# Two-layer graph kernel: the end of the last graph, with its roots regrouped and the work of the graph before moved forward

## The chip, the core and the metric

The kernel runs on one core of a Trainium2 chip. The metric is the device time of one execution in microseconds (us); lower is better. The core has five engines with queues of their own, each working through its queue in order: TensorE (PE, matrix products; PEld is its loading of weights), VectorE (DVE), ScalarE (ACT), GpSimd (POOL) and SyncE (SP, which here issues DMAs). They wait for each other by semaphores.

## The reference, cut to what matters

There are 16 graphs of 1024 nodes with 256 features. Two layers follow each other, and both end in a residual addition and a layer norm over the 256 features of a node. What matters for the change is the second layer's end and the layer norm:

```python
def _layernorm(x, axis=-1, eps=1e-5):
    m = jnp.mean(x, axis=axis, keepdims=True)
    v = jnp.var(x, axis=axis, keepdims=True)
    return (x - m) / jnp.sqrt(v + eps)
...
    Hh = jnp.einsum('bni,io->bno', h, W)
    logits = s[:, :, None] + d[:, None, :]
    e = jnp.where(adj != 0, jnp.exp(-leaky_relu(logits)), 0)
    rowsum = jnp.sum(e, axis=-1, keepdims=True)
    h_prime = jnp.einsum('bnm,bmo->bno', e, Hh) / rowsum
    return jax.nn.elu(h_prime)
...
x = _layernorm(x + _L0_gnn_ref(...))
x = _layernorm(x + _L1_gnn_ref(...))
```

So each output row is the norm of `x1 + elu(sum / rowsum)`, where `x1` is the row after the first layer.

## The kernel before, in words

The rows of a graph are eight tiles of 128. The kernel works through the graphs in a pipeline: while graph `b` runs through its first layer, the second layer of graph `b - 1` (`prev`) is finished, and the normed rows of graph `b - 2` (`done`) are scaled and stored. The schedule is written by hand (`tc.manual_schedule()`): each engine gets its instructions in the order in which the Python code emits them. This holds for the DMA queues too, since a DMA is issued in its place in an engine's queue.

A tile of the second layer passes through these steps. `sum1` (L654) accumulates the product of the weights `e` with `H` on TensorE, with the sum of a row's weights as a last column. `elu` takes its reciprocal on VectorE (L690, L691), and ScalarE makes the positive part (L699) and the exponential (L700). `add` joins both (L705) and adds `x1` (L707 for most graphs, L712 for graph 15), both on VectorE. Then the mean and the variance are needed. For most graphs the mean comes out of the addition, and `deviation1` has ScalarE sum the squares (L364). For graph 15, the last one, VectorE takes statistics of the row (`stats`: L346 and L348).

`center` makes the factor `r = 1/sqrt(v + eps)` and the offset `mr = -mean * r` for several tiles at once on GpSimd, in one batch of eight instructions: the sum with eps (L356 or L358), a power of -0.5 (L377), a Newton step of four instructions (L380 to L383), and the offset in two (L393, L394). `scale1` then has ScalarE scale a tile (L399), and `store` writes tiles out (L727) from SyncE's queue, or ScalarE's where it says so.

The end of the program begins in the last round of the loop (`last`, with `b` = 15 and `prev` = 14). There the eight tiles of graph 14 are summed; after tile 7's sums the weights of graph 15 for its first four tiles of rows are made on VectorE (`weights`, L649), eight of 128x512 followed by eight more for the second half. Then follow graph 15's own sums: the first four tiles together, over `m` from 0 to 7 (`acc_15_0` to `acc_15_3`), then tiles 4, 5 and 6, and last tile 7 in two halves of columns (L1046). Within this stretch VectorE adds tile 7 of graph 14, ScalarE takes the last two deviations, and GpSimd makes all eight roots of graph 14 (`center(mv1s[done])`). The eight scalings of graph 14 are spread, two after each of graph 15's tiles 2 to 5.

The tiles of graph 15 are rooted in this way: tiles 0 to 2 in one batch on GpSimd after tile 3's sums (code of `t == 4`), tiles 3 to 5 in a second batch (`t == 5`), and tiles 6 and 7 at the very end by a square root on ScalarE (L992) and a reciprocal with a Newton step on VectorE (L997 to L1002), which then also scales both tiles (L1119). The square root belongs to another set of activation tables than the exponentials, so ScalarE loads one ahead of it.

The kernel counts on all values of `adj` being 0 or 1 and on sums within limits. A flag is computed on the way (L1087), each engine loads it into a register (L1094), and a branch on it (L1463) decides between a general path, which does not run with these inputs, and the last store: tiles 6 and 7 of graph 15 from `y_last` (L1467, SyncE). After it all engines meet to close the program (L1501).

Of the kernel before, what the change touches and what calls it, by code (L numbers as in the profile page):

```python
# [18 lines left out]
P = 128  # L19
# [11 lines left out]
def one_kind_pass(  # L31
# [312 lines left out]
    def stats(y, mv, what):  # L344
        st = small.tile([P, nc.vector.BN_STATS_DIM], F32, tag="st", name=f"st_{what}")
        nc.vector.bn_stats(st, y)  # L346
        if mv is not None:
            nc.vector.bn_aggr(mv, st)  # L348
        return st
# [38 lines left out]
    def center(mv, what, add_eps=EPS, unit=1.0):  # L388

        r = rstd(mv, what, add_eps, unit)  # L390
        n = mv.shape[1]
        mr = small.tile([P, NT], F32, tag="mr", name=f"mr_{what}")[:, 0:n]
        nc.gpsimd.tensor_tensor(mr, mv[:, :, 0], r, ALU.mult)  # L393
        nc.gpsimd.tensor_scalar(mr, mr, -unit, None, ALU.mult)  # L394
        r_all[what] = r
        return [(r[:, t : t + 1], mr[:, t : t + 1]) for t in range(n)]
# [240 lines left out]
    def check_pq(b):  # L637
        near = small.tile([P, 2, NT], F32, tag="near", name=f"near_{b}")
        nc.vector.tensor_scalar(near, pqs[b], LOW, 1.0 / LOW, ALU.max, ALU.min)
        nc.vector.tensor_tensor(near, near, pqs[b], ALU.is_equal)  # L640
        nc.vector.tensor_reduce(fit[:, b : b + 1], near, AX.XY, ALU.min)

    def weights(b, m, t0=0, n=NT):

        if m == 0 and t0 == 0:
            es[b] = one.tile([P, NT, N], F32, tag="ew" if b < B - 1 else "al", name=f"e_{b}")
        cols = ds(t0 * P, n * P)
        q, e, rows = pqs[b][:, 1, m : m + 1], es[b][:, m, cols], adjs[b, m // HT][:, m % HT, cols]
        nc.vector.scalar_tensor_tensor(e, p_bcs[b][:, cols], q, rows, ALU.mult, ALU.min)  # L649
# [3 lines left out]
    def sum1(b, t, acc, m):  # L653
        nc.tensor.matmul(  # L654
            acc,
            lhsT=es[b][:, m, ts(t, P)],
            rhs=Hs[b][m],
            start=(m == 0),
            stop=(m == NT - 1),
        )  # L660
# [41 lines left out]
    def add(b, t, between=None):  # L702

        y = ys[b][t]
        nc.vector.scalar_tensor_tensor(y, y, 1.0, hs[b, t], ALU.min, ALU.add)  # L705
        if b < B - 1:
            nc.vector.scalar_tensor_tensor(  # L707
                y, y, -1.0, x1s[b][:, t, :], ALU.add, ALU.add, accum_out=mv1s[b][:, t, 0:1]
            )
            return None  # L710
        if (b, t) != (B - 1, NT - 2):
            nc.vector.scalar_tensor_tensor(y, y, -1.0, x1s[b][:, t, :], ALU.add, ALU.add)  # L712
        if between:
            between()

        full = (b, t) == (B - 1, NT - 2)
        return stats(y, None if full else mv1s[b][:, t, :], f"1_{b}_{t}")

    def deviation1(b, t):
        deviation(ys[b][t], mv1s[b][:, t, :])  # L720
# [82 lines left out]
    for b in range(1, B):  # L803
# [127 lines left out]
        for t in range(NT):  # L931
            if t == 6 and not last:
                add(prev, t - 1)
                deviation1(prev, t - 2)
                strip(b + 1, 0)
                finish(b + 1, 0, ends=False)
                dump(b + 1, 0)
            if t >= n_first:
                acc = sum_of(t)
                for m in range(NT):  # L940
                    sum1(prev, t, acc, m)
            if last and t == 7:
                for m in range(4):
                    weights(b, m, 0, HT)
            elu(prev, t, *((first[t], rinvs[t]) if t < n_first else (acc,)))
            if last and t in (2, 3):
                for q in range(HT):
                    stats0(b, (t - 2) * HT + q)
                roots0(b, t - 2)
            if t >= 1 and (last or t != 6):  # L950
                add(prev, t - 1)
            if t >= 2 and (last or t != 6):
                deviation1(prev, t - 2)
            if not last and t in (3, 5):
                sums0(b, (t - 3) // 2)
                if t == 5:
                    load_adj(b + 1, 1, behind=mv0s[b][:, HT, 0:1])
            if not last and t >= 4:
                for q in range(2 * t - 8, 2 * t - 6):
                    deviation0(b, q)  # L960
                if t % 2 == 1:
                    roots0(b, (t - 5) // 2)
            for n in ([0], [1], [2, 3])[t - 5] if not last and t >= 5 else []:
                combine_x(b + 1, n)
            if t == 3 and not last:
                scale_x(b + 1, 0)
                scale_x(b + 1, 1)
            if last and t in (4, 6):
                t0 = (t - 4) // 2 * HT
                for n in range(HT):  # L970
                    project(b, t0 + n)
                evict_H()
                save_p(b, t0, HT, nc.gpsimd)
                share_p(b, t0, HT)
            if last and t in (5, 7):
                for q in range(HT):
                    scale0(b, (t - 5) // 2 * HT + q)
            if last and t == 7:
                for m in range(4, 6):
                    weights(b, m, 0, HT)  # L980
# [4 lines left out]
    last, done = B - 1, B - 2  # L985
    r1s[last] = []

    def root(t, st):

        nc.vector.bn_aggr(mv1s[last][:, t, :], st)  # L990
        r = roots_sb[:, t - (NT - 2) : t - (NT - 2) + 1]
        nc.scalar.activation(r, mv1s[last][:, t, 1:2], AF.Sqrt, bias=eps)  # L992

    def invert_roots():

        v, r = mv1s[last][:, NT - 2 :, 1], roots_sb
        nc.vector.reciprocal(r, r)  # L997

        n = const.tile([P, 2], F32, tag="newton", name="newton")
        nc.vector.scalar_tensor_tensor(n, v, EPS, r, ALU.add, ALU.mult)  # L1000
        nc.vector.scalar_tensor_tensor(n, n, -0.5, r, ALU.mult, ALU.mult)
        nc.vector.scalar_tensor_tensor(r, n, 1.5, r, ALU.add, ALU.mult)  # L1002
        return r

    roots_sb = const.tile([P, 2], F32, tag="root", name="root")
    n_first = 4
    first = [acc1(last, t, *((ps_e, "e") if t < 3 else (ps_t, "t"))) for t in range(n_first)]
    for m in range(NT):
        if m in (3, 4):
            weights(last, m + 3, 0, HT)  # L1010
        if m == 4:
            add(done, NT - 1)
            for q in (NT - 2, NT - 1):
                deviation1(done, q)
            r1s[done] = center(mv1s[done], f"1_{done}", unit=1.0 / D)

        for k in range(3 * m - 15, min(3 * m - 12, NT)) if m >= 5 else []:
            weights(last, k, HT, HT)
        for t in range(n_first):
            sum1(last, t, first[t], m)  # L1020
    check_pq(last)

    n_chk, n_fit = chk.shape[1], fit.shape[1]
# [51 lines left out]
    for t in range(end):  # L1075
        if n_first - 1 <= t < end - 1:
            multiply1(t + 1)
        if t == 5:
            multiply_halves()
        if t == 4:  # L1080
            total = ps_t.tile([P, HT, P], F32, tag="t", name="total")[0:1, 0, 0:1]
            nc.tensor.matmul(total, lhsT=any_bad, rhs=ones, start=True, stop=True)
        elu(last, t, accs[t])
        if 1 <= t < 6:
            add(last, t - 1)
        if t == 5:
            nc.vector.tensor_copy(flag, total)  # L1087
            add(last, t)
        if t == 6:
            st_full = add(last, t, invert)  # L1090
        if t in (4, 5):
            r1s[last] += center(mv1s[last][:, ds(3 * t - 12, 3), :], f"1_{last}_{t}")
        if t == 5:
            n_bad = nc.values_load(  # L1094
                flag, min_val=0, max_val=P, skip_runtime_bounds_check_because="a number of partitions"
            )
        for q in range(2 * t - 4, 2 * t - 2) if 2 <= t < 6 else []:
            scale1(done, q)
            if q in (3, 7):
                store(done, q - 3, HT)  # L1100
        if t == 5:
            for q in range(3):
                scale1(last, q)
            store(last, 0, 3)
    h_end = two.tile([P, D], F32, tag="h", name="h_end")
    st_end = two.tile([P, 2, nc.vector.BN_STATS_DIM], F32, tag="low", name="st_end")
    end_half(0)
    scale1(last, 3)
    scale1(last, 4)
    store(last, 3, 2)  # L1110
    end_half(1)
    root(end, st_end)
    root(end - 1, st_full)
    r = invert_roots()
    scale1(last, 5)
    store(last, 5, 1, nc.scalar)
    for q in (6, 7):
        y = ys[last][q]
        nc.vector.tensor_scalar(  # L1119
            y, y, mv1s[last][:, q, 0:1], r[:, q - 6 : q - 5], ALU.subtract, ALU.mult  # L1120
        )
    return n_bad


# [380 lines left out]
```

## Time and profile before

| | |
|---|---|
| time, median of 3 runs | 1214.67 us (1214.66 to 1217.69) |
| the profiled execution's own time | 1215.24 us |
| its span, from first to last instruction | 1213.4 us |
| TensorE busy | 1202.4 us, 99% of the span |
| VectorE, ScalarE, GpSimd busy | 83%, 69%, 32% |
| TensorE's last product ends | 1205.1 us |
| the last store is issued (L1467) | 1209.42 us |
| mean granted TensorE clock | 0.998 |

The page gives the busy time of each engine, the span in 40 slices, and the chain of work that ended last. The timeline of one engine lists its instructions in order of time: start, duration, engine, line, operation, what it writes and reads, how often (xN), and in brackets the idle time before it with what ended it. The answer for one source line lists its instructions by queue (POOLq is GpSimd's instruction queue, which also takes the waits and branches), with the shortest, median and longest duration in ns, and when the first and the last of them start.

### The profile page before, as it was taken

To read this page: it belongs to the slowest core of one execution; us is meant where nothing else is said; L and a number is where in the kernel's file an instruction comes from. 1 tells how busy PE (TensorE), PEld (TensorE's weight loads), DVE (VectorE), ACT (ScalarE), POOL (GpSimd) and SP (SyncE) were. 2 spreads that over 40 slices of the span, in tenths; PEclk is the share of its full clock that TensorE was granted. 3 is DMA by queue.
4 is the path that set the end of the run, shared out by engine and by line. 5 is a ranking of instruction groups with operands and counts; after the bars stand their busy time and mean duration, and the time that the engine had idled before them with its cause. 6 is when DMAs were issued, how large, how long until landed. Compare 5 with 4: busy or idle time off the path is not lost.

```text
span 1213.4 us, 16001 instructions
## 1 busy us (share of the span) xinstructions
PE 1202.4 (99%) x4369; PEld 817.5 (67%) x4369; DVE 1005.8 (83%) x1778; ACT 833.2 (69%) x2133; POOL 391.2 (32%) x716
## 2 busy tenths in 40 slices
PE   9999999999999999999999999999999999999997
PEld 6757657576575766758667586775757657576686
DVE  5798896987979789797897978979798896988956
ACT  4574767767677666875768757786676767767674
POOL 3310433504334142431414324143250433404343
PEclk9999999999999999999999999999999999999999
DMA  9778788696887878788687886978869788687412
GB/s 201 150 147 156 131 157 171 132 190 127 149 176 135 184 146 154 157 144 182 139 176 134 153 183 129 182 138 155 174 131 190 129 154 172 133 188 135 112 49 73
DMA packets 613913, 182.51 MB, mean 150 GB/s; under 512 B 490164, under 2 KB 596280, under 8 KB 613816
## 3 DMA queue, kind: packets, MB, share of 16 engines
q1 hardware_dynamic: 591632, 138.74, 57.4%
q0 software_dynamic: 20528, 41.95, 18.6%
q8 instruction: 37, 0.61, 0.2%
q10 hardware_dynamic: 1656, 0.72, 0.2%
q14 instruction: 60, 0.49, 0.2%
HBM read 153.36 MB, written 61.54 MB: 177 GB/s over the span
## 4 chain that ended last, share of the span: by engine, by line
PE 93%; DVE 2%; DMA 2%; ACT 1%; SPq 1%; issue 1%; POOL 0%; ACTq 0%; DVEq 0%
PE acc L654 36%; PE pe L262 18%; PE pW L497 8%; PE pV L497 8%; PE pH L594 8%; PE pQ L497 8%; PE pR L497 4%; PE acc L416 2%; DMA al<-mir 1%; SPq L302 0%; DMA mir<-tb 0%; SPq L122 0%; DMA x_rows<-x 0%; PE busy L149 0%; DVE al L278 0%
## 5 line engine op out<-in xcount | busy, mean ns | idle before, releaser
L654 PE MATMUL acc<-H,e 128*128 128x257 f32 x2032 | 446.9, 380 | 0.0
L654 PEld LDWEIGHTS acc<-H,e 128*128 128x128 f32 x2032 | 385.0, 190 | 69.0 <-issue 13.9
L262 PE MATMUL pe<-xa,xT 128*128 128x384 f32 (+1 forms) x720 | 249.3, 486 | 0.1
L262 PEld LDWEIGHTS pe<-xa,xT 128*128 128x128 f32 x720 | 133.8, 190 | 91.7 <-issue 52.9
L649 DVE SCALAR_TENSOR_TENSOR e<-p,pq_kept,adj 128x1024 f32<-128x1024 f32 (+1 forms) x136 | 159.9, 1229 | 0.1
L292 POOL TENSOR_TENSOR al<-ident,al 128x128 f32<-128x128 f32 x128 | 109.1, 865 | 140.6 <-DVE al L278 140.5
L475 DVE TENSOR_TENSOR al<-al 128x1024 f32<-128x1024 f32 (+2 forms) x105 | 143.7, 1369 | 5.1
L272 DVE TENSOR_TENSOR tb<-tb,low 128x384 f32<-128x384 f32 (+1 forms) x180 | 105.8, 596 | 46.4 <-ACT low L271 44.8
L270 ACT ACTIVATE tb<-pe 128x384 f32<-128x384 f32 (+1 forms) x180 | 88.1, 489 | 57.7 <-PE pe L262 34.6
L130 ACT ACTIVATE junk<-adj,minus 128x2048 bf16<-128x2048 bf16 x64 | 127.3, 1990 | 0.1
L104 POOL CAST adj<-x 128x1 bf16<-128x1 f32 x15 | 3.1, 207 | 349.9 <-DMA x<-y_rows 274.2
L594 PE MATMUL pH<-Wx,yT 128*128 128x258 f32 x480 | 114.1, 380 | 0.0
L497 PE MATMUL pV<-al,S 128*128 128x512 f32 x240 | 108.5, 593 | 1.6 <-DVE al L475 1.6
L594 PEld LDWEIGHTS pH<-Wx,yT 128*128 128x128 f32 x480 | 91.1, 190 | 25.3 <-issue 6.7
L497 PE MATMUL pW<-al,x 128*128 128x512 f32 x240 | 107.9, 592 | 0.0
L497 PE MATMUL pQ<-al,x 128*128 128x512 f32 x240 | 107.9, 592 | 0.0
L325 DVE SCALAR_TENSOR_TENSOR al<-al,adj 128x512 f32<-128x512 f32 (+3 forms) x153 | 83.9, 564 | 18.7 <-DMA al<-mir 18.7
L699 ACT ACTIVATE h<-acc,rinv 128x256 f32<-128x256 f32 x81 | 38.1, 470 | 84.8 <-DVE rinv L691 74.9
L680 ACT ACTIVATE sums<-acc,tiny 128x1 f32<-128x1 f32 x45 | 11.8, 261 | 122.2 <-PE acc L654 122.2
L271 ACT ACTIVATE low<-pe 128x512 f32<-128x512 f32 (+1 forms) x192 | 94.9, 495 | 0.0
L278 DVE SCALAR_TENSOR_TENSOR al<-tb,adj 128x1024 f32<-128x1024 f32 (+3 forms) x120 | 90.9, 758 | 4.5
L399 ACT ACTIVATE y_kept<-y_kept,mr,r 128x256 f32<-128x256 f32 x120 | 64.9, 589 | 30.1 <-POOL mr L394 28.9
(149 smaller groups left out, 1658.9 us busy)
## 6 DMA issues: line engine op xcount, KB each, us to landing
adj<-in_adjT POOLq DMA_DIRECT2D x30, 1024.0 KB, 8.4
x<-in_x SPq DMA_DIRECT2D x15, 1024.0 KB
y_rows<-Z SPq DMA_DIRECT2D x240, 64.0 KB
x<-y_rows SPq DMA_DIRECT2D x30, 512.0 KB
out<-y_kept SPq DMA_DIRECT2D x30, 512.0 KB
xT<-in_x SPq DMA_DIRECT2D x112, 128.0 KB
p<-p_row POOLq DMA_DIRECT2D x15, 512.0 KB, 4.1
mir<-tb SPq DMA_DIRECT2D x60, 112.0 KB
```

The costliest lines, as they stand in the source:

```text
L130: nc.scalar.activation(junk, rows, AF.Square, bias=minus1, scale=2.0, accum_out=chk[:, b * CHECKS + n : b * CHECKS + n + 1],)
L262: nc.tensor.matmul(pe[:, 0:w], lhsT=xTs[b][:, c, ts(jt, P)], rhs=xas[b][:, c, ds(jt * P + o, w)], start=(c == 0), stop=(c == ND - 1),)
L270: nc.scalar.activation(tb[:, ds(o, w)], pe[:, 0:w], AF.Tanh, scale=0.5)
L271: nc.scalar.activation(low[:, 0:w], pe[:, 0:w], AF.Tanh, scale=0.5 * SLOPE)
L272: nc.vector.tensor_tensor(tb[:, ds(o, w)], tb[:, ds(o, w)], low[:, 0:w], ALU.max)
L278: nc.vector.scalar_tensor_tensor(als[b][:, jt, c0:c1], tbs[b, jt][:, c0 - jt * P : c1 - jt * P], 1.0, adjs[b, jt // HT][:, jt % HT, c0:c1] ...
L292: nc.gpsimd.tensor_tensor(diag, ident2, diag, ALU.add)
L475: nc.vector.tensor_tensor(out_, in0, in1, ALU.subtract)
L497: nc.tensor.matmul(banks[bank], lhsT=lhs[:, jt, :], rhs=rhs[:, jt, :], start=first and jt == 0, stop=jt == HT - 1, skip_group_check=True,)
L594: nc.tensor.matmul(pt, lhsT=x1Ts[b][:, c, ts(t, P)], rhs=Wx[:, c, :], start=(c == 0), stop=(c == ND - 1),)
L649: nc.vector.scalar_tensor_tensor(e, p_bcs[b][:, cols], q, rows, ALU.mult, ALU.min)
L654: nc.tensor.matmul(acc, lhsT=es[b][:, m, ts(t, P)], rhs=Hs[b][m], start=(m == 0), stop=(m == NT - 1),)
```

## The change

- `add` takes the mean and variance of tile 6 of graph 15 at once, as for the other tiles.
- In the last round, the addition of graph 14's tile 6 is put ahead of graph 15's first weights, and that of tile 7 ahead of the weights for `m` = 6. Graph 14's batch of roots is emitted with it.
- A load of the table set that holds both logarithm and exponential follows graph 14's last deviation on ScalarE.
- Seven of graph 14's scalings are put ahead of graph 15's tile 0, the eighth after tile 1, and its two stores with them.
- The roots of graph 15 on GpSimd: tiles 0 to 2 are emitted one tile earlier; tiles 3 and 4, tile 5, and tile 6 become batches of their own. Tile 5's batch stands ahead of GpSimd's load of the flag, tile 6's behind it.
- Tile 6 is scaled on ScalarE, tile 7 alone on VectorE. Tile 7's root is `exp(-0.5 * ln(v + eps))` on ScalarE and the same Newton step.
- The scalings of tiles 3 and 4 go ahead of tile 7's first half on ScalarE, tile 5's scaling and its store ahead of tile 7's logarithm.

```diff
@@ add
-        full = (b, t) == (B - 1, NT - 2)
-        return stats(y, None if full else mv1s[b][:, t, :], f"1_{b}_{t}")
+        return stats(y, mv1s[b][:, t, :], f"1_{b}_{t}")
@@ last round of the loop over graphs
             if last and t == 7:
+                add(prev, t - 1)
                 for m in range(4):
                     weights(b, m, 0, HT)
...
-            if t >= 1 and (last or t != 6):
+            if t >= 1 and t != (7 if last else 6):
                 add(prev, t - 1)
@@ roots of the last tiles
-    def root(t, st):
-
-        nc.vector.bn_aggr(mv1s[last][:, t, :], st)
-        r = roots_sb[:, t - (NT - 2) : t - (NT - 2) + 1]
-        nc.scalar.activation(r, mv1s[last][:, t, 1:2], AF.Sqrt, bias=eps)
-
-    def invert_roots():
-
-        v, r = mv1s[last][:, NT - 2 :, 1], roots_sb
-        nc.vector.reciprocal(r, r)
-
-        n = const.tile([P, 2], F32, tag="newton", name="newton")
+    def root():
+
+        mv = mv1s[last][:, NT - 1, :]
+        nc.vector.bn_aggr(mv, st_end)
+        v, r = mv[:, 1:2], const.tile([P, 1], F32, tag="root", name="root")
+        nc.scalar.activation(r, v, AF.Ln, bias=eps)
+        nc.scalar.activation(r, r, AF.Exp, scale=-0.5)
+
+        n = const.tile([P, 1], F32, tag="newton", name="newton")
         nc.vector.scalar_tensor_tensor(n, v, EPS, r, ALU.add, ALU.mult)
...
-    roots_sb = const.tile([P, 2], F32, tag="root", name="root")
...
     for m in range(NT):
-        if m in (3, 4):
-            weights(last, m + 3, 0, HT)
-        if m == 4:
+        if m == 3:
             add(done, NT - 1)
             for q in (NT - 2, NT - 1):
                 deviation1(done, q)
             r1s[done] = center(mv1s[done], f"1_{done}", unit=1.0 / D)
+            nc.scalar.preload_act_table_set("natural_log_exp_and_others")
+        if m in (3, 4):
+            weights(last, m + 3, 0, HT)
...
+    for q in range(NT - 1):
+        scale1(done, q)
+        if q == 3:
+            store(done, 0, HT)
     check_pq(last)
@@ the loop over graph 15's tiles t
         if t == 6:
-            st_full = add(last, t, invert)
-        if t in (4, 5):
-            r1s[last] += center(mv1s[last][:, ds(3 * t - 12, 3), :], f"1_{last}_{t}")
+            add(last, t, invert)
+        if t == 1:
+            scale1(done, NT - 1)
+            store(done, HT, HT)
+        for t0, n in {3: [(0, 3)], 5: [(3, 2), (5, 1)], 6: [(6, 1)]}.get(t, []):
+            r1s[last] += center(mv1s[last][:, ds(t0, n), :], f"1_{last}_{t0}")
         if t == 5:
             n_bad = nc.values_load(
...
-        for q in range(2 * t - 4, 2 * t - 2) if 2 <= t < 6 else []:
-            scale1(done, q)
-            if q in (3, 7):
-                store(done, q - 3, HT)
-        if t == 5:
             for q in range(3):
                 scale1(last, q)
             store(last, 0, 3)
+    for q in (3, 4):
+        scale1(last, q)
+    store(last, 3, 2)
...
     end_half(0)
-    scale1(last, 3)
-    scale1(last, 4)
-    store(last, 3, 2)
     end_half(1)
-    root(end, st_end)
-    root(end - 1, st_full)
-    r = invert_roots()
     scale1(last, 5)
     store(last, 5, 1, nc.scalar)
-    for q in (6, 7):
-        y = ys[last][q]
-        nc.vector.tensor_scalar(
-            y, y, mv1s[last][:, q, 0:1], r[:, q - 6 : q - 5], ALU.subtract, ALU.mult
-        )
+    r = root()
+    scale1(last, NT - 2)
+    y = ys[last][end]
+    nc.vector.tensor_scalar(y, y, mv1s[last][:, end, 0:1], r, ALU.subtract, ALU.mult)
     return n_bad
```

## The prediction

> **What bounds the kernel now.** I read the page first: its span line, its engines, its chain of work.
>
> ```profile
> span 1213.4 us, 16001 instructions
> PE 1202.4 (99%) x4369; PEld 817.5 (67%) x4369; DVE 1005.8 (83%) x1778; ACT 833.2 (69%) x2133; POOL 391.2 (32%) x716
> ```
>
> TensorE is busy for 99%, so nothing that the change touches can move more than the end: TensorE's own order is untouched, and its last product ends at 1205.1. The profiled execution took 1215.24 us, 1.84 more than its span and 0.57 more than the median of the three timed runs (1214.67); I add differences of the span to the median. 0.3% of it, about what a measurement of this kernel can tell from no change, is 3.6 us.
>
> So I read the timeline of single engines from 1157 us on. ScalarE around graph 15's first tile:
>
> ```profile
> 1182.16 0.51 ACT L364 ACTIVATE dev_junk<-y_kept,mv 128x256 bf16<-128x256 f32 x1 [0.46 <-DVE y_kept L707]
> ...
> 1189.93 0.47 ACT L699 ACTIVATE h<-acc,rinv 128x256 f32<-128x256 f32 x1 [7.17 <-PE acc L654]
> ...
> 1206.06 1.28 ACT L992 ACT_TABLE_LOAD   x1
> 1207.36 0.48 ACT L992 ACTIVATE root<-mv,eps 128x1 f32<-128x1 f32 x2
> ```
>
> ScalarE idles 7.17 us before tile 0, and loads a table on the chain at the very end. GpSimd's three batches of roots in this stretch, first and last instruction of each:
>
> ```profile
> 1182.86 0.19 POOL L358 TENSOR_SCALAR ve<-mv 128x8 f32<-128x8 f32 x1 [3.51 <-ACT dev_junk L364]
> ...
> 1188.02 0.25 POOL L394 TENSOR_SCALAR mr<-mr 128x8 f32<-128x8 f32 x1
> 1195.85 0.24 POOL L356 TENSOR_SCALAR ve<-mv 128x3 f32<-128x3 f32 x1 [7.57 <-DVE rinv L690]
> ...
> 1198.59 0.43 POOL L394 TENSOR_SCALAR mr<-mr 128x3 f32<-128x3 f32 x1
> 1201.17 0.23 POOL L356 TENSOR_SCALAR ve<-mv 128x3 f32<-128x3 f32 x1 [2.16 <-DVE mv L348]
> ...
> 1204.00 0.25 POOL L394 TENSOR_SCALAR mr<-mr 128x3 f32<-128x3 f32 x1
> ```
>
> A batch of three tiles takes 3.17 and 3.08 us; graph 14's eight tiles take 5.41. Last I read what follows GpSimd's work: the load of the flag (L1094), the branch on it (L1463) and the close (L1501).
>
> ```profile
> L1094 POOLq TENSOR_LOAD <-flag x1: 777/777/777, 1204.0 to 1204.0; - x1
> ```
>
> ```profile
> L1463 POOLq EVENT_SEMAPHORE  x5: 17/43/43, 1207.5 to 1207.8; - x5
> ...
> L1463 POOLq COMPARE_BRANCH  x1: 45/45/45, 1204.8 to 1204.8; - x1
> ...
> L1463 POOLq INC_SWDGE_SEM  x1: 732/732/732, 1207.9 to 1207.9; - x1
> ```
>
> ```profile
> L1501 POOLq DRAIN  x3: 46/107/2273, 1208.7 to 1213.2; - x3
> L1501 SPq DRAIN  x3: 7/7/7, 1212.6 to 1212.9; - x3
> ```
>
> GpSimd branches at 1204.80; its next instruction is at 1207.50 (2.7 later), then come 0.4 of semaphores, 0.73, and a drain of 2.27 that starts at 1208.7: it is ready to close at 1210.95, 6.15 us after its branch. SyncE, with the last store (issued at 1209.42), arrives only at 1212.6, and 0.8 later the span ends. GpSimd thus has 1.7 us to spare there, and the change puts two more batches ahead of its branch.
>
> **The change part by part.**
>
> Graph 14's additions. Tile 6's two (0.42 each) go ahead of the weights, so tile 7's reciprocal, and its ELU on ScalarE (1177.92), come 0.88 later. ScalarE loses its wait of 0.46 for tile 7's addition in return: the last deviation moves by about +0.3, and so does graph 14's batch of roots, to 1183.2 to 1188.6. The first weights of graph 15 then end at about 1176.4 instead of 1175.5. TensorE wants them after 16 records of 0.22 from 1173.12, at 1176.6, less a weight load of 0.19: 0 to 0.3 us of stall. I take it as nothing: VectorE and ScalarE run behind TensorE from there on (below); were they not, it would cost these 0.3.
>
> Graph 14's scalings. Seven now stand ahead of tile 0's ELU in ScalarE's queue, waiting for that batch. Four take 1.97 (1179.14 to 1181.11), so seven take 3.45: tile 0's ELU starts at 1192.05 instead of 1189.93, 2.1 us late. SyncE's two stores of graph 14 go earlier, ahead of anything that waits there. Behind the ELU wait VectorE's additions: tile 0's at 1192.9 (was 1190.81), then 1.70 each (1190.81, 1192.52, 1194.22). Before, VectorE idled 0.28 and 0.46 for TensorE at tiles 5 and 6; these absorb part. Tile 4's addition starts at 1199.7 instead of 1198.02 and its statistics end 1.57 later, at 1201.3.
>
> GpSimd. The batch of tiles 0 to 2 follows tile 2's statistics (1197.9 to 1201.1). By columns the power takes 1.95 for eight, 1.04 for four, 0.885 for three: falling by 0.16 to 0.23 a column, so at 0.16 a batch of two takes 2.97, and one of one tile 2.47 from its first to its last instruction's start (2.79 for three). Lower end 0.23 a column, 0.4 less in all; upper end no saving at all, 0.8 more. Tiles 3 and 4: 1201.4 to 1204.35. Tile 5: 1204.4, last instruction at 1206.9. Flag load (0.78, started as the batch's last instruction does) and a gap of 0.07: 1207.7. Tile 6: last instruction at 1207.7 + 2.47 = 1210.15, end 1210.4. The branch stood 0.07 behind the flag load; now nothing stands between, so it goes at 1210.15, 5.35 later than before.
>
> Exit. 1210.15 + 6.15 = 1216.3, and 0.8 for the close: the span ends at 1217.1, 3.7 later. For the step from branch to next instruction the other engines' rows give 0.46 (SyncE) to 3.8 (TensorE); I take GpSimd's own 2.7. The drain's other two rows are 0.05 and 0.11; no row shows what the long one waits for, so I keep 0.1 as its lower end and take 2.27, its own.
>
> Tile 7 and the last store. VectorE reaches tile 6's reciprocal at 1203.2 (was 1201.55; its flag load of 0.54, once beside TensorE, is now bare), and everything of tiles 6 and 7 follows about 1.5 late: statistics of tile 7 end at 1208.5. Logarithm and exponential (two of 128x1 at about 0.29 with their hand-over), three Newton steps at 0.195, one scaling of 0.41: ScalarE is free for them only at 1208.6, behind tile 5's scaling and the issue of its store (0.38), so tile 7 is done at about 1210.3. Removed are the table load (which costs 0.4, from 1206.99 to 1207.36, since the rest lies beside statistics), a reciprocal, the second root and the second scaling: 0.8 of the 2.7 from statistics to store. The load moves into ScalarE's idle time before graph 14's roots, where 5 us hide it. But the store holds tile 6 too, scaled on ScalarE after GpSimd: 1210.45 to 1211.05. Issued at 1211.07 instead of 1209.42: +1.65.
>
> The later of the two exits decides: +3.7 against +1.65. So 1214.67 + 3.7 = 1218.4.
>
> Two rules against the trace. The table load's row is 1.28 and the next activation starts 1.30 after it does. The Trainium skill's page "ScalarE: Activation LUTs", section "What ACT_TABLE_LOAD costs", gives 1.28 and a drain of 1.38, 2.66 for each switch of set. By the page the removal would be worth 1.4 more on tile 7's path, and since that is not the later exit the sum would still be 1218.4. Beside the weights, GpSimd's small steps took 0.57 to 0.59 (from 1185.7 to 1187.6), but 0.19 to 0.25 mostly beside VectorE's additions, where the batch of tiles 0 to 2 ran. The page "SBUF — State Buffer", section "SBUF: two separate sides", speaks against the change here: VectorE with two SBUF inputs and a GpSimd step that reads SBUF exclude each other for a whole instruction. Taken so for half of the three later batches' steps at 0.2 a step, an estimate from that page, the sum would be some 2.4 higher, 1220.8; the row of the batch decides for me.
>
> **The rivals.**
>
> The exit is short: the drain is not tied to GpSimd's branch, and the last store, held by tile 6's scaling, ends the span: 1214.67 + 1.65 = 1216.3, not slower by the bound. It decides if the drain falls below 0.2. For it: two drains of 0.1 and less; against: the long one began 0.03 behind GpSimd's own previous instruction.
>
> The tail gets faster: had GpSimd branched before 1206.5 and graph 14's roots been ready by 1186.4, tile 0 would not wait and the 0.8 is won: 1213.9. Against: its second batch cannot start before tile 4's statistics, and three batches and the flag load behind it take 8.8.
>
> GpSimd is slowed: tiles 3 to 6 at the rate seen beside the weights, 0.66 from step to step instead of 0.28, for five steps of three batches: +5.7 on top, 1224. For it the rows at 1185.7; against the batch of tiles 0 to 2.
>
> **How the numbers follow.** GpSimd's exit sets the end: 0.70, with 3.7 between 2.9 (0.4 by columns, 0.4 by the ELU's lateness) and 5.6 (0.8 by columns, 1.1 for a branch as long as TensorE's), so 1217.6 to 1220.3; two thirds of it are over the bound at 1218.3, as its long side lies above. Short exit: 0.14, 1216.3. Faster tail: 0.05, within the bound at 1213.9, though 0.02 of it beyond. GpSimd slowed: 0.11. Slower 0.47 + 0.11 = 0.58; faster 0.02; same 0.40. The range leaves out the faster tail and the slowed GpSimd: 1216.3 less 0.5 for the ELU's lateness, to 1220.5, the first case's long end rounded up.
>
> **What would show it.** Right: seven scalings ahead of tile 0's ELU near 1192; GpSimd's batches back to back from 1201.4 to 1210.4, its branch near 1210.2, its long drain ending near 1216.3, SyncE's arrival about 2 us before that. The last store near 1211.1, and no table load after 1185. Wrong: a GpSimd that arrives before SyncE, a drain that shrinks, or a tile 0 that starts before 1191.

## The result, and the profile after

The changed kernel took 1218.55 us (median of 13 runs), the kernel before 1215.22 us (median of 13 runs on the same chip). The ratio is 1.003 with a 95% interval of 1.0023 to 1.0037: slower by 3.3 us, between 2.8 and 4.5. The prediction was 1218.4 us, with the cause that GpSimd's exit becomes the last one. That the two times lie within 0.2 us is luck: the prediction started from 1214.67, the median of three runs, 0.55 below the median of thirteen, and its rise of 3.7 was 0.4 too large.

The profiled execution of the changed kernel took 1219.66 us. The head of its page:

```profile
span 1217.8 us, 16019 instructions
## 1 busy us (share of the span) xinstructions
PE 1203.0 (99%) x4369; PEld 817.8 (67%) x4369; DVE 1006.1 (83%) x1776; ACT 834.1 (68%) x2134; POOL 394.8 (32%) x732
```

The span is 4.4 us longer. Of that, 0.49 lies ahead of everything that the change touches: TensorE's last long run of products begins at 1173.61 instead of 1173.12. Wherever I compare with a time of the prediction, I take 0.49 off. GpSimd has 16 instructions more, which are two batches.

ScalarE's timeline after (start, duration, engine, line, what, and in brackets the idle time before and its releaser):

```profile
1183.64 1.28 ACT L1010 ACT_TABLE_LOAD   x1
1189.34 3.55 ACT L399 ACTIVATE y_kept<-y_kept,mr,r 128x256 f32<-128x256 f32 x7 [4.42 <-POOL mr L394]
1192.79 0.45 ACT L699 ACTIVATE h<-acc,rinv 128x256 f32<-128x256 f32 x1
...
1209.32 0.29 ACT L993 ACTIVATE root<-mv,eps 128x1 f32<-128x1 f32 x1 [0.46 <-DVE mv L991]
1209.65 0.20 ACT L994 ACTIVATE root<-root 128x1 f32<-128x1 f32 x1
1211.00 0.60 ACT L399 ACTIVATE y_last<-y_last,mr,r 128x256 f32<-128x256 f32 x1 [1.15 <-POOL mr L394]
```

The wait of 7.17 us ahead of tile 0 has become a wait of 4.42 for GpSimd and seven scalings, and tile 0 starts later than before. The last line is tile 6's scaling: it waits for GpSimd, at the place where VectorE did both tiles before. GpSimd's timeline after, first and last instruction of each batch and the two powers of one column:

```profile
1183.72 0.66 POOL L358 TENSOR_SCALAR ve<-mv 128x8 f32<-128x8 f32 x1 [3.89 <-ACT dev_junk L364]
...
1189.06 0.24 POOL L394 TENSOR_SCALAR mr<-mr 128x8 f32<-128x8 f32 x1
1198.68 0.24 POOL L356 TENSOR_SCALAR ve<-mv 128x3 f32<-128x3 f32 x1 [9.38 <-DVE rinv L690]
...
1201.73 0.25 POOL L394 TENSOR_SCALAR mr<-mr 128x3 f32<-128x3 f32 x1
1202.09 0.37 POOL L356 TENSOR_SCALAR ve<-mv 128x2 f32<-128x2 f32 x1
...
1204.87 0.24 POOL L394 TENSOR_SCALAR mr<-mr 128x2 f32<-128x2 f32 x1
1205.18 0.23 POOL L356 TENSOR_SCALAR ve<-mv 128x1 f32<-128x1 f32 x1
1205.49 0.82 POOL L377 TENSOR_TENSOR r<-ve,power 128x1 f32<-128x1 f32 x1
...
1207.79 0.24 POOL L394 TENSOR_SCALAR mr<-mr 128x1 f32<-128x1 f32 x1
1208.39 0.22 POOL L356 TENSOR_SCALAR ve<-mv 128x1 f32<-128x1 f32 x1 [0.36 <-ACT y_last L1071]
1208.69 0.57 POOL L377 TENSOR_TENSOR r<-ve,power 128x1 f32<-128x1 f32 x1
...
1210.73 0.24 POOL L394 TENSOR_SCALAR mr<-mr 128x1 f32<-128x1 f32 x1
```

From 1202.09 on GpSimd works through three batches with nothing between them but the load of the flag ahead of the last. The idle time of 0.36 that the view puts down to ScalarE there is mostly that load: it ends at 1208.24, and the batch begins 0.15 later. In nogen_a below the step from load to batch is as long (0.14), though ScalarE's L1071 had ended before the load did. The branch (L1458 now), the flag (L1098), the close (L1496) and the last store (L1462), from the answers for these lines (count, shortest/median/longest duration in ns, start of the first and of the last):

```profile
L1098 POOLq TENSOR_LOAD <-flag x1: 497/497/497, 1207.7 to 1207.7; - x1
```

```profile
L1458 POOLq EVENT_SEMAPHORE  x5: 17/43/43, 1213.5 to 1213.8; - x5
...
L1458 POOLq COMPARE_BRANCH  x1: 45/45/45, 1210.7 to 1210.7; - x1
...
L1458 POOLq INC_SWDGE_SEM  x1: 732/732/732, 1213.9 to 1213.9; - x1
```

```profile
L1496 POOLq DRAIN  x3: 46/107/2273, 1214.7 to 1217.5; - x3
L1496 SPq DRAIN  x3: 7/7/7, 1215.7 to 1217.2; - x3
```

```profile
L1462 SPq DMA_DIRECT2D out<-y_last x1: 373/373/373, 1211.6 to 1211.6; - x1
```

GpSimd branches at 1210.7, issues its next instruction at 1213.5, and begins its long drain at 1214.7; 2.27 later, at 1217.0, it is ready, and the span ends at 1217.8. SyncE arrives at 1215.7. Before, the order was the other way round: GpSimd ready at 1211.0, SyncE at 1212.6.

### The profile page after: what moved, and what is told of

It reads as the page before. It is cut to its first block, busy times and chain, and to the rows that moved or that the text cites. A ratio compares the mean times of both kernels' runs of the same rounds, so it can differ in the third digit from the quotient of the medians.

```text
span 1217.8 us, 16019 instructions
## 1 busy us (share of the span) xinstructions
PE 1203.0 (99%) x4369; PEld 817.8 (67%) x4369; DVE 1006.1 (83%) x1776; ACT 834.1 (68%) x2134; POOL 394.8 (32%) x732
## 4 chain that ended last, share of the span: by engine, by line
PE 92%; DVE 2%; DMA 2%; ACT 1%; SPq 1%; issue 1%; POOL 0%; ACTq 0%; DVEq 0%; POOLq 0%
PE acc L654 35%; PE pe L262 18%; PE pW L497 8%; PE pV L497 8%; PE pH L594 8%; PE pQ L497 8%; PE pR L497 4%; PE acc L416 2%; DMA al<-mir 1%; SPq L302 0%; DMA x<-in_x 0%; SPq L122 0%; DMA x_rows<-x 0%; DVE al L278 0%; ACT dev_junk L364 0%
## 5 line engine op out<-in xcount | busy, mean ns | idle before, releaser
L594 PE MATMUL pH<-Wx,yT 128*128 128x258 f32 x480 | 114.1, 380 | 0.0
L594 PEld LDWEIGHTS pH<-Wx,yT 128*128 128x128 f32 x480 | 91.1, 190 | 25.3 <-issue 6.7
```

What stands on the lines that cost most here:

```text
L594: nc.tensor.matmul(pt, lhsT=x1Ts[b][:, c, ts(t, P)], rhs=Wx[:, c, :], start=(c == 0), stop=(c == ND - 1),)
```

## The experiments

**The theory**: two arrivals close the program, GpSimd's (its branch, about 3 us to its next instruction, 0.4 of semaphores, 0.73, a drain of 2.27) and SyncE's, behind the last store; the span ends 0.8 after the later one. **The rivals**: that the late store alone accounts for the loss, or that TensorE, VectorE or ScalarE lost time through the moved scalings and additions.

In the table all times are those of one profiled execution of each kernel, counted from the start of the last of the L594 products, at 1172.75 in the profile of the kernel before; the change does not touch the time of what comes before it. "GpSimd ready" is the end of its long drain, "SyncE arrives" the start of the second of its three drains at the close; "none" says that GpSimd goes from the branch straight to its drain. "Against before" is the difference of the medians on the same chip, with the interval worked out from that of the ratio.

| kernel | GpSimd branches | to its next instruction | GpSimd ready | last store issued | SyncE arrives | span ends | against before, us |
|---|---|---|---|---|---|---|---|
| before | 32.06 | 2.69 | 38.20 | 36.67 | 39.88 | 40.69 | |
| changed | 37.45 | 2.84 | 43.73 | 38.39 | 42.57 | 44.57 | +3.3 (2.8 to 4.5) |
| pool4 | 33.11 | 3.19 | 39.76 | 36.65 | 39.92 | 40.73 | +0.1 (-1.1 to 1.2) |
| pool16 | 36.74 | 3.04 | 43.24 | 36.66 | 42.08 | 44.07 | +2.8 (1.8 to 4.3) |
| spread | 35.63 | 3.26 | 42.35 | 36.58 | 41.18 | 43.19 | +2.5 (1.3 to 3.8) |
| six | 34.80 | 2.54 | 40.80 | 37.72 | 40.94 | 41.76 | +1.5 (0.4 to 2.7) |
| spread_six | 33.22 | 2.54 | 39.23 | 36.15 | 39.99 | 40.81 | 0.0 (-1.2 to 1.0) |
| sqrt | 37.41 | 2.89 | 43.76 | 38.94 | 42.59 | 44.60 | +3.8 (1.9 to 4.9) |
| nogen_a | 37.88 | none | 40.46 | 38.82 | 41.45 | 42.28 | +1.6 (0.1 to 2.4) |
| nogen_b | 32.07 | none | 34.51 | 36.66 | 39.62 | 40.45 | +0.5 (-0.9 to 1.5) |
| lnexp | 32.05 | 2.75 | 38.27 | 36.17 | 40.04 | 40.86 | +0.2 (-1.0 to 1.2) |
| best | 31.91 | 2.68 | 38.04 | 35.99 | 39.54 | 40.36 | -0.5 (-1.8 to 0.4) |

In every row the span ends 0.8 after the later of the two arrivals.

**A late GpSimd by itself: pool4 and pool16.** The kernel before, with small steps that nobody reads between GpSimd's load of the flag and its branch:

```diff
+    idle = const.tile([P, 1], F32, tag="idle", name="idle")
+    nc.gpsimd.memset(idle, 0.0)
+    for _ in range(16):     # 4 in pool4
+        nc.gpsimd.tensor_scalar(idle, idle, 1.0, None, ALU.mult)
```

> The kernel before, with five small dependent steps put on GpSimd behind its second batch of roots, ahead of its branch (one memset of 128x1 and four scalings of it; their result is not used). By the exit theory GpSimd has 1.7 us to spare before the close: at some 0.28 a step its branch moves by about 1.3, its long drain ends near 1212.3 instead of 1210.95, SyncE still arrives last, at about 1212.6, and the time stays that of before (0 to +0.3 us). By the rival that the last store alone decides it stays too, so this run only sets the lower side of the slack.

> The same with one memset and sixteen scalings, 4.6 to 4.8 us of GpSimd work that nobody waits for. Exit theory: the branch moves by 4.7, the drain keeps its 2.27 and ends near 1215.6, later than SyncE, and the time rises by 4.7 - 1.7 = 3.0 us (2.6 to 3.4). Rival of the short exit or of the last store: the last store is issued at the same time, and the time does not move (0 to +0.3).

GpSimd's timeline in pool16 and the answers for its branch (L1468), close (L1506) and last store (L1472):

```profile
1204.27 4.72 POOL L1109 TENSOR_SCALAR idle<-idle 128x1 f32<-128x1 f32 x16
```

```profile
L1468 POOLq COMPARE_BRANCH  x1: 45/45/45, 1208.7 to 1208.7; - x1
```

```profile
L1506 POOLq DRAIN  x3: 46/107/2273, 1213.0 to 1215.8; - x3
L1506 SPq DRAIN  x3: 7/7/7, 1214.0 to 1215.5; - x3
```

```profile
L1472 SPq DMA_DIRECT2D out<-y_last x1: 373/373/373, 1208.7 to 1208.7; - x1
```

The last store is where it was (36.66 against 36.67 in the table), nothing else was touched, and the kernel is 2.8 us slower; 3.0 were expected. Five steps (pool4) cost nothing that can be measured (+0.1, interval -1.1 to 1.2): GpSimd's ready time of 39.76 still lies ahead of SyncE's 39.92. So a GpSimd that is late at its branch, by more than its 1.7 us to spare, is enough for a loss of this size, without any change on the other engines.

**Which part of the change makes it late: spread, six and spread_six.** In spread, the changed kernel has graph 14's scalings where the kernel before has them, two after each of the tiles 2 to 5. In six, GpSimd's batch for tile 6 is gone; the root of tiles 6 and 7 is the logarithm and exponential over two columns, and VectorE scales both. spread_six does both.

```diff
 spread
-    for q in range(NT - 1):
-        scale1(done, q)
...
+        for q in range(2 * t - 4, 2 * t - 2) if 2 <= t < 6 else []:
+            scale1(done, q)
 six
-        for t0, n in {3: [(0, 3)], 5: [(3, 2), (5, 1)], 6: [(6, 1)]}.get(t, []):
+        for t0, n in {3: [(0, 3)], 5: [(3, 2), (5, 1)]}.get(t, []):
...
-    scale1(last, NT - 2)
...
+    for q in (6, 7):
```

> The changed kernel with graph 14's eight scalings put back where they were (two after each of tiles 2 to 5 of graph 15) and all the rest of the change kept. Exit theory: tile 0's ELU goes back by about 2.4 us, tile 4's statistics by 1.9, GpSimd's four batches with them, and the time falls by 1.9 against the changed kernel (1.5 to 2.2), that is to +1.2 to +1.8 over the kernel before, since GpSimd still branches last. Rival that lateness of tile 0 alone made the change slow, by way of the last store: all of +3.3 is gone (-0.8 to +0.3 against the kernel before).

> The changed kernel with tile 6's root taken off GpSimd: tiles 6 and 7 take logarithm, exponential and Newton step together in two columns, and VectorE scales both; seven scalings stay ahead of tile 0. Exit theory: GpSimd branches right behind its load of the flag, 2.4 us sooner than in the changed kernel, and the time falls by 2.0 to 2.5 against it, to +0.8 to +1.4 over the kernel before. Rival of the last store: the store goes only about 0.4 sooner, and the time falls by 0.4 (+2.9 over the kernel before).

> Both together on the changed kernel: scalings of graph 14 spread as before, and tile 6's root with tile 7's, off GpSimd. Exit theory: GpSimd branches near 1206.1 on the profile's time of before, and ends its drain near 1212.4; the last store goes near 1209.2. The two exits are about level, and the time is that of the kernel before (-0.4 to +0.4). If something else of the change costs time (the additions of graph 14, the smaller batches, the moved table load), it stays over the kernel before by more than 0.5.

Tile 0 on ScalarE in spread, and GpSimd's first instruction for tile 6 there:

```profile
1189.68 0.47 ACT L699 ACTIVATE h<-acc,rinv 128x256 f32<-128x256 f32 x1 [5.49 <-PE acc L654]
```

```profile
1205.80 0.22 POOL L356 TENSOR_SCALAR ve<-mv 128x1 f32<-128x1 f32 x1 [0.61 <-ACT y_last L1067]
```

Tile 0 now waits for TensorE again, and no longer for scalings. That regained 0.8 us of the 3.3 by the medians, and the theory asked for 1.5 to 2.2: the expectation missed. The table gives a part of the reason. The branch came 1.82 sooner than in the changed kernel, near the 1.9 that were expected, but the step from the branch to the next instruction took 3.26 instead of 2.84, so GpSimd was ready only 1.38 sooner. (The 0.61 ahead of tile 6's batch is again mostly the load of the flag, 0.74 here, and not ScalarE.) The rest, between these 1.38 and the 0.8, is a difference between single executions and medians; the intervals of the two medians (2.8 to 4.5 and 1.3 to 3.8) overlap, and no run tells more. The last store is back at its place before (36.58 against 36.67), and still the kernel loses 2.5 us: a rival that blames the store is excluded by this run as by pool16.

Without tile 6's batch 1.5 of the loss are left, close to the expected 0.8 to 1.4, and the two arrivals nearly meet (40.80 and 40.94). SyncE's is the later one here, behind a store that is issued 1.05 later than before: with the scalings ahead of tile 0 both arrivals are late, so what is left in six is not GpSimd's exit alone. With both parts undone no loss can be measured (0.0, interval -1.2 to 1.0), although graph 14's additions, the smaller batches and the moved table load are still there: no loss of theirs is seen. So two things make the loss, the seven scalings ahead of tile 0 and a fourth batch ahead of the branch, and each alone is enough for one. Their prices do not add up: undoing one gains 0.8, undoing the other 1.8, undoing both 3.3, since the later of two arrivals decides.

**The table load: sqrt and lnexp.** sqrt is the changed kernel with the square root and its table load back at the end; lnexp is the kernel before with logarithm and exponential over both columns, and the load in ScalarE's idle time.

```diff
 sqrt
-            nc.scalar.preload_act_table_set("natural_log_exp_and_others")
-        nc.scalar.activation(r, v, AF.Ln, bias=eps)
-        nc.scalar.activation(r, r, AF.Exp, scale=-0.5)
+        nc.scalar.activation(r, v, AF.Sqrt, bias=eps)
+        nc.vector.reciprocal(r, r)
 lnexp: the other way round, in the kernel before
```

> The changed kernel with tile 7's root by square root and reciprocal, so that the table load goes back to ScalarE's end and the one in the idle time is gone. Exit theory: the last store is issued about 0.5 us later than in the changed kernel (table load of 1.28, of which the rest lies beside statistics), but GpSimd's exit stays last by some 0.7, and the time is that of the changed kernel (-0.2 to +0.2, so +3.3 over the kernel before). Rival of the last store: +0.5 on the changed kernel.

> The kernel before with the root alone changed: tiles 6 and 7 by one logarithm and one exponential over two columns, the table load moved to ScalarE's idle time behind graph 14's last deviation. The last store goes 0.5 us sooner (0.37 of waiting for the table, a reciprocal of 0.2 and a second root of 0.2 less, one exponential of 0.3 more), and GpSimd's exit, 1.7 ahead, does not bind: -0.5 us (-0.7 to -0.2). Rival that the page's drain of 1.38 at a switch of tables was on the path: -1.8.

In sqrt the store is issued 0.55 later than in the changed kernel, and the end does not move (44.60 against 44.57; the medians, +3.8 and +3.3, have intervals that overlap widely): what GpSimd's exit covers costs nothing. In lnexp the store is issued 0.50 sooner than before, which is the gain by the row of the load; but SyncE arrives no sooner (40.04 against 39.88), and the median says +0.2 where -0.5 was expected. SyncE's waits say where the 0.50 went (the kernel before, lnexp, and best, which follows below):

```profile
SPq L1463 <- SPq L1463: 1.0, 1, 1.0
```

```profile
SPq L1463 <- SPq L1463: 1.8, 1, 1.8
```

```profile
SPq L1462 <- SPq L1462: 1.4, 1, 1.4
```

SyncE stands behind the issue of its last store, ahead of the semaphores that it resets, until 38.01 in the kernel before and 38.34 in lnexp on the table's clock. The view names SyncE itself as what ended the wait, but the semaphore that SyncE waits for first there is that of ScalarE's store of tile 5, and by the trace's semaphore events the last part of that store landed 0.02 earlier, at 37.99 and 38.32. It is so, within 0.02, in all six kernels in which this store lands behind the issue of the last one (before, pool4, pool16, six, lnexp, best); in the other four that have these semaphores (changed, spread, spread_six, sqrt) it has landed by then, and SyncE does not stand there. So the landing of another store held SyncE, and in lnexp it came later though that store was issued 0.30 sooner. Why, no run shows. (The last store's own transfer took longer too, 2.84 us instead of 2.33, but SyncE asks for it only afterwards and did not wait for it in lnexp.) ScalarE's root in lnexp:

```profile
1208.05 0.29 ACT L995 ACTIVATE root<-mv,eps 128x2 f32<-128x2 f32 x1 [0.97 <-DVE mv L990]
1208.38 0.20 ACT L996 ACTIVATE root<-root 128x2 f32<-128x2 f32 x1
```

Ahead of the logarithm no load stands any more, only the wait for VectorE's statistics, and 0.33 later the exponential follows.

The Trainium skill's page "ScalarE: Activation LUTs", section "What ACT_TABLE_LOAD costs", puts a drain of 1.38 on top of the load's 1.28. An estimate from that page, with the 0.4 of the load that lay on the path, is that removing it brings the store 1.8 sooner. It came 0.50 sooner, so in this place the drain is not seen.

**The length of the exit: nogen_a and nogen_b.** The general path, which does not run with these inputs, is replaced by a single store of tiles that does not run either; nogen_a does so in the changed kernel, nogen_b in the kernel before. The branch itself stays, over this store (nogen_b's expectation counts it as gone).

```diff
         with tc.If(n_bad > 0) as found:
-            general_pass(tc, x, adjT, a0, a1, a2, a3, bias, W, a, out)
+            rows = out[0].rearrange("(t p) d -> p t d", p=P)
+            nc.sync.dma_start(rows[:, 0:N_LAST, :], y_last)
```

> The changed kernel without its general path: in place of that path, which does not run with these inputs, the branch's first side holds one store. Theory that the 2.7 to 2.8 us between GpSimd's branch and its next instruction are the fetch of code that lies far off, behind the general path: that step falls below 0.6 us, GpSimd's drain ends 2.2 sooner, SyncE arrives last, and the time falls by 1.2 to 2.2 against the changed kernel. Rival that a branch costs this however far it goes: the step stays 2.7 and the time that of the changed kernel (+3.3 over the kernel before).

> The kernel before without the branch and the general path, which does not run with these inputs; the last store stands in their place. Theory (later of the two exits): GpSimd, whose branch, semaphores and long way to the next instruction go, comes to its closing drain about 3.5 us sooner, and that is worth nothing by itself, since SyncE came last already; SyncE's own wait on GpSimd's resets goes too, so 0 to -0.6 us. Rival (the general path's exit costs every end its length): -1.7 us, as it was worth in the changed kernel.

GpSimd's branch and close in nogen_a (L1458, L1497):

```profile
L1458 POOLq COMPARE_BRANCH  x1: 45/45/45, 1209.6 to 1209.6; - x1
```

```profile
L1497 POOLq DRAIN  x3: 46/113/2407, 1209.8 to 1213.7; - x3
L1497 SPq DRAIN  x3: 7/7/7, 1213.1 to 1213.4; - x3
```

The close in nogen_b (L1502):

```profile
L1502 POOLq DRAIN  x3: 46/107/2273, 1204.5 to 1212.5; - x3
L1502 SPq DRAIN  x3: 7/7/7, 1211.8 to 1212.2; - x3
```

In nogen_a it is 0.17 from the branch to the long drain (4.0 in the changed kernel): the wait for the next instruction, the semaphores and the 0.73 are all gone. The edit takes away the long path and what GpSimd resets behind it together, so the run does not tell if the 2.8 us to the next instruction come from the distance of the jump, as its expectation supposes. The drain stays, at 2.41. GpSimd is ready at 40.46, SyncE at 41.45 comes last, and what is left of the loss is +1.6 (0.1 to 2.4). With GpSimd's exit out of the way, then, the late store does cost time, as the prediction's rival of the short exit has it. That its +1.65 is met so closely is partly luck: the store is issued 2.15 later than before here, and SyncE arrives 2.63 behind it instead of 3.21.

In the kernel before the same edit makes GpSimd ready 3.7 sooner and is worth nothing that can be measured (+0.5, interval -0.9 to 1.5), since SyncE came last there already. The same 4 us are bound in one kernel and free in the other.

**A version that takes the good parts: best.** The kernel before, with the root of lnexp, tile 6's aggregate at once, and graph 14's scalings spread so that none delays an ELU; GpSimd's three batches stay.

```diff
+        for q in {1: (3, 4), 2: (5, 6), 3: (7,)}.get(t, ()):     # three more stand ahead of tile 0
+            scale1(done, q)
...
+            nc.scalar.preload_act_table_set("natural_log_exp_and_others")
```

> The kernel before with these parts: tile 6's statistics are aggregated at once, the root of tiles 6 and 7 is an exponential of a logarithm whose table load lies in ScalarE's idle time after graph 14, graph 14's scalings stand three ahead of tile 0, two after tile 1, two after tile 2 and one after tile 3, and the scalings of tiles 0 to 2 go ahead of the flag. GpSimd's three batches and its branch stay where the kernel before has them. Theory (what binds is the later of GpSimd's exit and SyncE's arrival behind the last store): GpSimd branches near its old place (32.0 us behind the start of the last of the L594 products in the kernel before), the last store is issued about 0.7 us sooner (36.67 there, so 36.0), and the span ends with it: -0.2 to -0.9 us against the kernel before. Rival (SyncE's arrival hangs on the chain of semaphores and landings and not on the issue of the store, as the run with logarithm and exponential alone suggests): 0, within 0.3 us either way.

The close of best, and its last store:

```profile
L1500 POOLq DRAIN  x3: 46/107/2273, 1208.0 to 1212.4; - x3
L1500 SPq DRAIN  x3: 7/7/7, 1211.8 to 1212.1; - x3
```

```profile
L1466 SPq DMA_DIRECT2D out<-y_last x1: 372/372/372, 1208.3 to 1208.3; - x1
```

The store is issued 0.68 sooner than before (35.99 against 36.67), as expected, but SyncE arrives only 0.34 sooner. As in lnexp, SyncE first stands until tile 5's store from ScalarE has landed (37.78, and SyncE goes on at 37.80). The medians differ by -0.5 us, and the interval (-1.8 to 0.4) holds no change too. Set against the changed kernel's +3.3 it is some 3.8 us faster; that it beats the kernel before isn't shown.

## Why the prediction was right, step by step

- **Graph 14's additions** ahead of the weights: taken as no stall for TensorE. TensorE's chain runs on from 1173.61 without a gap, and graph 15's tile 7 starts 0.48 later than before (1201.82 against 1201.34), which is the shift that was there already. Right. Graph 14's batch was put at 1183.2 to 1188.6 and came, less the shift, at 1183.2 to 1188.8.
- **The seven scalings**: 3.45 from their start to tile 0's ELU, as predicted. The ELU came at 1192.30 (less the shift) instead of 1192.05, the 0.2 of the batch ahead of it.
- **GpSimd's batches**: right in their order and in their sum, less so one by one. A batch of one column was put at 2.47 from its first to its last instruction; tile 5 took 2.61 and tile 6 2.34. The power, which I let fall by 0.16 a column, took 0.90 for three columns, 0.87 for two, and for one 0.82 (tile 5) and 0.57 (tile 6). The load of the flag took 0.50 instead of 0.78, and from its end to tile 6's batch it was 0.15 instead of 0.07. These errors cancel: the branch came at 1210.19 (less the shift) where the text has 1210.15. That this is within 0.04 is luck; errors of 0.1 to 0.3 in the terms are what such rows allow.
- **The rival of a slowed GpSimd**: its price, +5.7, came from GpSimd's steps of 0.57 to 0.59 beside the weights; the Trainium skill's page "SBUF — State Buffer", section "SBUF: two separate sides", by which a VectorE instruction with two SBUF inputs and a GpSimd step that reads SBUF exclude each other, stood behind an estimate of its own, 2.4. Beside the weights graph 14's batch had such steps again (0.58 and 0.59, and 0.22 for the first step after the weights had ended); in the four batches of graph 15, beside VectorE's additions of 256 columns, the steps between the powers took 0.19 to 0.38, and the estimate's 2.4 are not seen. Right to weigh it low.
- **The exit**: 6.15 from branch to ready were predicted. They were 6.28, 0.15 more from branch to next instruction, and the drain of 2.27 to the nanosecond. I had left open if the drain is GpSimd's own; pool16 and nogen_a show that it follows GpSimd's branch wherever that stands, and in nogen_b its 2.27 are over, at 34.51, before the last store is issued at 36.66.
- **Tile 7 and the last store**: put at 1211.07, found at 1211.13 (less the shift); that it has a price shows in nogen_a, +1.6, there for a store 2.15 late. What I had not seen is that SyncE, too, waits for GpSimd. SyncE's waits in the changed kernel (engine and line, releaser: us in total, times, longest):

```profile
SPq L1496 <- DMA p_row<-pT: 2.1, 1, 2.1
...
SPq L1462 <- ACT y_last L399: 0.7, 1, 0.7
```

The second line is the store that waits for tile 6's scaling. The first is at the close; p_row is the transfer in GpSimd's own queue, long landed, so it stands for something else that came late. In the four kernels in which GpSimd is ready last by far (changed, pool16, spread, sqrt) this wait ends 0.68 after GpSimd's 0.73 step has begun, at 41.38 against 40.70 in the changed kernel. With the general path out (nogen_a) step and wait are gone and SyncE arrives 1.1 sooner, although its store was issued 0.43 later: SyncE's arrival is tied to GpSimd's exit. The two arrivals, which I treated as independent, are only partly so: SyncE's was to come about 2 us ahead of GpSimd's and came 1.2 ahead. It did not matter here, since GpSimd's own came last.

- **The sum**: +3.7 predicted, +3.3 measured by medians; the profiles differ by 3.9 from the mark of the table. The step from branch to next instruction, which I took as fixed, varies between 2.54 and 3.26 from one kernel to the next; a spread as large as this difference.

## What to carry to other kernels

The end of a program is a race of arrivals, not of work: the engine whose busy time ends last need not be the one that ends the program, since each has its own way from its last instruction to the close, 6.2 us for GpSimd here against 3.2 from the last store for SyncE (2.6 to 3.9 in the kernels in which SyncE came last). Before work is moved to an idle engine at the end, add that way to the end of its work; an engine at 32% had only 1.7 us to spare. And a gain ahead of an arrival that isn't the last one, like the table load here, cannot be seen in the time, however cleanly the trace shows it. An arrival, too, can wait for several things: SyncE's waited here for GpSimd, for its own last store, or for another engine's store.

## What the runs showed of the hardware that was not expected

- GpSimd's step from the branch to its next instruction takes 2.54 to 3.26 us when it jumps over the general path, and, with semaphores and the 0.73 step, vanishes (0.17 to the drain) when one store stands in that path's place. Which of the two, the jump or the resets, makes the step was not tried. The closing drain on GpSimd takes 2.27 us in all runs but one (2.41).
- A last store that is issued 0.5 to 0.7 sooner brought SyncE's arrival forward by 0.34 in best and not at all in lnexp. SyncE went on 0.02 after ScalarE's store of tile 5 had landed in both, which took 2.65 and 3.01 us from its issue against 2.38 in the kernel before. What makes that landing slower is open.
- GpSimd's power of one column took 0.57 in one batch and 0.82 in another of the same kernel. What slowed the second was not tried.
